# Where layer norms, a reload and two gelus stand in the queues of a macaron transformer block

## The chip, the core and the metric

The kernel runs on one core of one Trainium2 chip. The metric is the device time of one execution in microseconds (us); less is better. Engines are named as in the profile: PE is TensorE (PEld its weight loads), DVE is VectorE, ACT is ScalarE, POOL is GpSimd, and SP is the engine that issues nearly all of the DMAs.

## The reference

One block of 2048 tokens with 512 features: half a gated MLP, causal attention with 16 heads of 32, and the same half MLP again. Every part is preceded by a layer norm without learnt weights. The MLP's weights come as 4-bit codes with one scale per 32 values, and both MLPs use the same weights.

```python
x = x + 0.5 * ffn(layernorm(x), gate_codes, gate_scales, up_codes, up_scales, down_codes, down_scales)
x = x + attn(layernorm(x), w_qkv, b_qkv, w_out, b_out)
x = x + 0.5 * ffn(layernorm(x), ...)          # the same weights again

def ffn(x, ...):                               # hidden width 4096
    gate, up = x @ Wg.T, x @ Wu.T              # Wg, Wu, Wd dequantised from the codes
    inter = gelu_tanh(gate) * up
    return inter @ Wd.T
def layernorm(x): return (x - mean(x)) / sqrt(var(x) + 1e-5)
```

All of it is float32.

## The kernel before, in words

The program is written out in one order by hand: the Python code emits instructions one after another, each goes to the end of its engine's queue, and no scheduler moves it. A line that is emitted earlier therefore stands earlier in its engine's queue and ahead of everything else that this engine has to do. Waits between engines are semaphores.

**The products.** Matrix products are done by Strassen-like schemes with seven half-size products in place of eight. Their sums are made by DVE, ACT and POOL around PE, out of seven rotating PSUM banks (pool `ps_one`, tag `one`) and one further bank (`ps_acc`).

**Transposition.** A product needs the normalised tokens with features on partitions. So each tile of 128 tokens is normalised by ACT (`normalize`: line 146, tile `xn`; in the second MLP's second half line 953, in place in tile `xl`), transposed by four PE instructions (line 155 into `pt_f` or `pt_a`; line 961 into `pt_later`), and copied out of its bank by ACT (line 156 into `xT`; line 962). Tiles `xn` and `xl` have two buffers each.

**First MLP, `ffn(1, ...)`.** Groups g = 0 to 7 of 512 hidden units; in each, `slot(...)` runs fourteen products for the gate (`pg`, line 339) and the up projection (`pu`), over a pair of blocks of 512 tokens. Token blocks 0 and 1 are normalised at the very start. Blocks 2 and 3 are normalised and transposed inside the second slot (`slot(g, second, 0, [], [], 1, late)`): after each product one group of the list `late` is emitted, and its first nine groups come from `staggered(n2, n3)`. In a slot ACT also copies products 1 and 5 out of their banks (lines 378 and 390) and applies the gelu to the four gate results (line 359), each after a DVE addition (line 381 for the first, `c`; then 392, 396, 399).

**Between the first MLP and attention.** `norms_behind` builds the same staggered list for attention's blocks 0 and 1; its groups stand behind the last fourteen pieces of the down projection (`po`, line 438).

**Second MLP, `second_ffn`.** It works on two halves of 1024 tokens. A half is 56 pairs of products (NP = 56; `pair(n, ...)`, n from 0 to 111), each with seven steps for the inner products y = 1, 5, 2, 6, 7, 3, 4. Their results `d`, `f`, `e` (line 746) share banks: y = 6, 7 and 4 accumulate on the bank of y = 1, so PE may start y = 7 only after ACT has copied the bank after y = 6 (`u2`, line 776). `hooks` holds further work by pair and step, `at(half, n, step, ...)`; step k is emitted after inner product k. Down pieces (`pod`, `pof`, `poe`, line 877, with ACT's copy of line 900 and DVE's line 886) are mixed in. Weights for pair n + 4 are fetched by six DMAs of SP when pair n ends (`fetch`, lines 620 to 622).

**The second half's tokens** have lain in DRAM (`away`). Their moments are computed early in the first half. `Later` then reloads the eight tiles (`load`, line 670, 256 KB each), normalises and transposes them while pairs 54 and 55 run. Tile i + 2 is loaded once transposition i has released its buffer.

**The end.** After pair 111 the loop body of n = 112 emits what is left, by hand: the `sums` of the last pair (DVE, line 800), its two `gelus` (ACT, line 803), the `gated` products (DVE, line 812), the sums for the down projection (DVE, lines 856 to 859), and between them the down pieces. A piece is named here by i and q. Left over from group 6 are (4,1), (5,1) and (3,1); fourteen of group 7 follow. Piece (3,1) accumulates on the bank that ACT's copy of (5,1) reads (line 900), and it is the last reader of the tile `s`, which line 856 writes anew.

## Time and profile before

| | |
|---|---|
| median of 3 runs | 3159.78 us (3156.42, 3159.78, 3159.99) |
| the profiled execution | 3161.12 us; its span 3159.3 us, so 1.8 us lie around the span |
| PE busy | 3114.4 us of the span (99%) |
| DVE / POOL / ACT busy | 2055.9 / 1534.8 / 1047.2 us |
| mean granted TensorE clock | 0.997 |

The span is the time that the profile covers, and all positions below are us from its start. "Busy" counts the time in which an engine has an instruction running. The granted clock is the share of full speed at which PE's array was clocked. Rows of a timeline give start, duration, engine, line, operation, and in brackets the idle time ahead of it with what ended it.

### The profile page before, as it was taken

Reading aid. Unit: us, or ns where it says so; the run is one execution under the profiler, and the core shown is the slowest. Engines: PE = TensorE matmul, PEld = TensorE weight load, DVE = VectorE, ACT = ScalarE, POOL = GpSimd, SP = SyncE. Lnnn points to the kernel's source line nnn. Section 1 sums busy time; section 2 is a strip of 40 time slices with the busy share of each in tenths; the row PEclk is TensorE's granted clock in tenths of the full one; section 3 lists DMA queues with packets and bytes.
Section 4 is the critical chain, followed back from the end, with each engine's and each line's share of the span. In section 5 each row is a group of like instructions: output and inputs, shape, how many; then the busy total and the mean of one; then the engine's idle time right before and its main releaser. Section 6 shows DMA issues by size and latency. Waiting matters only on the chain.

```text
span 3159.3 us, 45153 instructions
## 1 busy us (share of the span) xinstructions
PE 3114.4 (99%) x16592; PEld 2006.8 (64%) x16592; DVE 2055.9 (65%) x3182; ACT 1047.2 (33%) x2070; POOL 1534.8 (49%) x1529
## 2 busy tenths in 40 slices
PE   7999999999999999999999999999999999999998
PEld 4556565656565565444335434478888878888887
DVE  6666666666666655655564566687666777666775
ACT  5111111111111122355453456443333343333332
POOL 3767675857667672456564467522232223223221
PEclk9999999999999999999999999999999999999999
DMA  3223122212122220000000000064444445344441
GB/s 140 79 85 114 67 97 90 97 60 97 64 93 80 83 87 24 5 14 9 12 9 7 29 20 11 1 203 130 124 127 129 125 131 171 116 124 129 130 122 61
DMA packets 261293, 260.21 MB, mean 82 GB/s; under 512 B 21216, under 2 KB 225616, under 8 KB 257104
## 3 DMA queue, kind: packets, MB, share of 16 engines
q1 hardware_dynamic: 261072, 257.33, 25.0%
q8 instruction: 131, 2.15, 0.3%
q14 instruction: 90, 0.74, 0.1%
HBM read 176.28 MB, written 79.92 MB: 81 GB/s over the span
## 4 chain that ended last, share of the span: by engine, by line
PE 93%; DVE 2%; ACT 1%; POOL 1%; issue 1%; DMA 1%; SPq 0%; ACTq 0%; POOLq 0%; DVEq 0%
PE po L438 12%; PE d_f L746 12%; PE pg L339 12%; PE pu L339 12%; PE av L1278 7%; PE pod_f L877 7%; PE pm L1206 6%; PE f_f L746 6%; PE pqk L1122 4%; PE pof_f L877 3%; PE e_f L746 3%; PE ps L1357 2%; PE pv L1139 2%; PE pp L1159 2%; PE poe_f L877 2%; PE ps L1366 1%
## 5 line engine op out<-in xcount | busy, mean ns | idle before, releaser
L1391 ACT ACTIVATE pt<-ps 128x512 f32<-128x512 f32 (+3 forms) x608 | 288.2, 528 | 180.8 <-PE ps L1366 118.5
L1206 PE MATMUL pm<-kT,qT 32*128 32x512 f32 (+3 forms) x1280 | 332.3, 572 | 0.0
L1218 DVE TENSOR_REDUCE parts<-pm 128x1 f32<-128x512 f32 x384 | 246.6, 686 | 129.3 <-PE pm L1206 128.9
L746 PE MATMUL d_f<-ys_f,ring 128*128 128x256 f32 x1216 | 319.8, 384 | 10.1 <-DVE o_f L779 5.8
L1415 POOL TENSOR_TENSOR sum<-pt,pt 128x512 f32<-128x512 f32 (+1 forms) x225 | 265.9, 1202 | 95.2 <-ACT pt L1391 88.1
L1366 PE MATMUL ps<-qT,kT 32*128 32x512 f32 (+3 forms) x1280 | 278.3, 536 | 0.0
L746 PEld LDWEIGHTS d_f<-ys_f,ring 128*128 128x128 f32 x1216 | 226.4, 190 | 58.2 <-DVE o_f L779 21.3
L438 PEld LDWEIGHTS po<-wd,inter 128*128 128x128 f32 x1024 | 194.4, 190 | 77.5 <-issue 55.7
L800 DVE TENSOR_TENSOR o_f<-o_f,o_f 128x1024 f32<-128x1024 f32 x128 | 203.6, 1601 | 61.2 <-ACT o_f L785 56.5
L438 PE MATMUL po<-wd,inter 128*128 128x256 f32 x1024 | 241.1, 379 | 0.0
L339 PE MATMUL pg<-xT_f,w 128*128 128x512 f32 x512 | 240.6, 598 | 0.0
L339 PE MATMUL pu<-xT_f,w 128*128 128x512 f32 x512 | 238.0, 592 | 0.0
L892 POOL TENSOR_TENSOR xq<-xq,d_f 128x512 f32<-128x512 f32 x48 | 63.7, 1326 | 314.6 <-DVE xq L886 229.4
L452 POOL TENSOR_TENSOR xq<-xq,d 128x512 f32<-128x512 f32 x124 | 161.8, 1315 | 92.5 <-DVE xq L446 56.2
L892 POOL TENSOR_TENSOR xq_second<-xq_second,d_f 128x512 f32<-128x512 f32 x45 | 61.6, 1370 | 279.6 <-DVE xq_second L886 210.9
L1278 PE MATMUL av<-pt,vals 128*32 128x256 f32 (+1 forms) x2432 | 191.5, 369 | 2.4 <-ACT both L1300 2.3
L393 POOL TENSOR_TENSOR u<-u,u 128x512 f32<-128x512 f32 x64 | 81.9, 1279 | 211.1 <-ACT u L390 210.4
L438 PEld LDWEIGHTS po<-wd,s 128*128 128x128 f32 x768 | 145.5, 190 | 57.9 <-issue 39.2
L438 PE MATMUL po<-wd,s 128*128 128x256 f32 x768 | 181.4, 379 | 0.0
L339 PE MATMUL pg<-xsum,w 128*128 128x512 f32 x384 | 179.6, 597 | 0.0
L800 POOL TENSOR_TENSOR o_f<-o_f,o_f 128x1024 f32<-128x1024 f32 x44 | 119.2, 2709 | 123.8 <-ACT o_f L785 122.7
L339 PE MATMUL pu<-xsum,w 128*128 128x512 f32 x384 | 177.7, 592 | 0.0
(225 smaller groups left out, 6345.9 us busy)
## 6 DMA issues: line engine op xcount, KB each, us to landing
wd_f<-kept SPq DMA_DIRECT2D x112, 256.0 KB
kept<-wd SPq DMA_DIRECT2D x8, 1792.0 KB
xq<-in_x SPq DMA_DIRECT2D x16, 256.0 KB
pk<-in_gate_codes SPq DMA_DIRECT2D x16, 256.0 KB
sc<-in_gate_scales SPq DMA_DIRECT2D x32, 128.0 KB
pk<-in_up_codes SPq DMA_DIRECT2D x16, 256.0 KB
sc<-in_up_scales SPq DMA_DIRECT2D x32, 128.0 KB
pk<-in_down_codes SPq DMA_DIRECT2D x16, 256.0 KB
```

Source lines behind the costliest of these rows:

```text
L339: nc.tensor.matmul(ps, lhsT=a[:, j, :], rhs=b[:, j, :], start=(j == 0), stop=(j == 1))
L438: nc.tensor.matmul(ps[:, j, :], lhsT=a[i][:, k, bass.ts(2 * q + j, P)], rhs=b[i][:, k, :], start=(k == 0), stop=(k == 1),)
L452: adder.tensor_tensor(dst, dst, other, ALU.add)
L746: nc.tensor.matmul(ps[:, k, :], lhsT=fa[k][y], rhs=fb[k][y], start=first and k == 0, stop=True, skip_group_check=True,)
L800: sums.append(lambda: eng.tensor_tensor(dst, dst, other, ALU.add))
L877: nc.tensor.matmul(ps[:, j, :], lhsT=a[:, k, bass.ts(2 * q + j, P)], rhs=wd[:, PLACE[i], k, :], start=new and j == k == 0, stop=True, skip ...
L1206: nc.tensor.matmul(ps[a][:, :n], lhsT=q[r, bass.ts(4 * g + i, P)], rhs=k[r, kb * 512 : kb * 512 + n], start=True, stop=True,)
L1218: nc.vector.tensor_reduce(most, scores, AX.X, ALU.max)
L1278: nc.tensor.matmul(dst_, lhsT=lhsT, rhs=rhs, start=kw.get("start", False), stop=True, skip_group_check=True)
L1366: nc.tensor.matmul(ps[a][:, off:], lhsT=k[r, bass.ts(c, P)], rhs=q[r, g * 512 + off : (g + 1) * 512], start=False, stop=True,)
L1391: nc.scalar.activation(pt[:, a, plain[a] :], ps[a][:, plain[a] :], AF.Exp, scale=scale)
L1415: eng.tensor_tensor(s[:, a, off_2:], one[:, a, off_2:], other[:, a, off_2:], ALU.add)
```

## The change

Three places of the order are edited. The computation, the tiles and the number of instructions stay the same; PE's queue differs only in the place of four of the eight `pt_later` transpositions, the queues of DVE and POOL not at all.

1. `staggered`: the first group normalises two tiles in place of one, and each following group transposes tile i first and normalises tile i + 2 after it. Before, a group normalised tile i + 1 and then transposed tile i. The transpositions keep their groups. The function serves the first MLP (blocks 2 and 3) and attention (blocks 0 and 1).
2. `Later`: the loads of tiles 0 and 1 move from pair 52, step 5 to pair 30, step 0. The eight transpositions, before at steps 0, 2, 4, 6 of pairs 54 and 55, are now at steps 0, 2, 4, 6 of pair 54 and 1, 3, 5, 6 of pair 55. The load of tile i + 2 stays with transposition i. Normalisation i + 1, before in the same step as transposition i, now stands one step behind it.
3. The end: the two gelus of the last pair move behind pieces (5,1) of group 6 and (1,0) of group 7.

```diff
     def staggered(a, b):
         n, t = a.normal + b.normal, a.transposed + b.transposed
-        return [[n[0]]] + [[n[i + 1], t[i]] for i in range(7)] + [[t[7]]]
+        return [n[:2]] + [[t[i], n[i + 2]] for i in range(6)] + [[t[6]], [t[7]]]
...
-            at(0, 52, 5, call(later.load, 0), call(later.load, 1))
+            at(0, 30, 0, call(later.load, 0), call(later.load, 1))
             at(0, 53, 5, call(later.normalize, 0))
             for i in range(8):
-                place = 0, 54 + i // 4, 2 * (i % 4)
-                at(*place, call(later.transpose, i))
+                place = min(2 * i, 13)
+                at(0, 54 + place // 7, place % 7, call(later.transpose, i))
                 if i + 2 < 8:
-                    at(*place, call(later.load, i + 2))
+                    at(0, 54 + place // 7, place % 7, call(later.load, i + 2))
                 if i + 1 < 8:
-                    at(*place, call(later.normalize, i + 1))
+                    at(0, 54 + (place + 1) // 7, (place + 1) % 7, call(later.normalize, i + 1))
...
                     pieces.pop(0)()
-                    for f in sums + gelus:
+                    for f in sums:
                         f()
                     for piece in (pieces.pop(0), pieces.pop(1)):
                         piece()
-                    for f in gated + down_sums[:2]:
+                    for f in gelus + gated + down_sums[:2]:
                         f()
```

## The prediction

> **What bounds the kernel now.** The page says PE, and so does the chain that ended last (its shares by engine):

> ```profile
> PE 3114.4 (99%) x16592; PEld 2006.8 (64%) x16592; DVE 2055.9 (65%) x3182; ACT 1047.2 (33%) x2070; POOL 1534.8 (49%) x1529
> ...
> PE 93%; DVE 2%; ACT 1%; POOL 1%; issue 1%; DMA 1%; SPq 0%; ACTq 0%; POOLq 0%; DVEq 0%
> ```

> The change removes no PE work, so it can only win idle PE time (44.9 us in all) or slow PE time. PE's own list of waits (total, times, longest) names three that lie where the edits are:

> ```profile
> PE pt_f L155 <- ACT xn_f L146: 14.6, 5, 9.4
> ...
> PE d_f L746 <- ACT u_f L776: 4.1, 2, 2.2
> PE pof_f L877 <- ACT d_f L900: 3.5, 2, 2.8
> ```

> 9.4 us of the first is the start of the program, which no edit touches. I then read PE's timeline at each place, and ACT's beside it. Place A, the second slot of the first MLP:

> ```profile
> 56.25 1.13 PE L155 MATMUL pt_f<-ident,xn_f 128*128 128x128 f32 x4 [3.25 <-ACT xn_f L146]
> 57.17 3.62 PE L339 MATMUL pg<-xsum,w 128*128 128x512 f32 x4
> ```
> ```profile
> 49.66 0.82 ACT L146 ACTIVATE xn_f<-xq,nbias_f,rstd_f 128x512 f32<-128x512 f32 x1
> 54.86 0.63 ACT L359 ACTIVATE c<-c 128x512 f32<-128x512 f32 x1 [4.38 <-DVE c L381]
> 55.40 0.80 ACT L146 ACTIVATE xn_f<-xq,nbias_f,rstd_f 128x512 f32<-128x512 f32 x1
> ```

> ACT stood idle for 4.38 us ahead of a gelu whose input DVE had not made, with the next norm queued behind it; PE waited for that norm. The product after it took 3.62 us where its neighbours take 1.88. The table by stretches (length, busy us of PE, PEld, DVE, ACT, POOL, then granted clock) tells why:

> ```profile
> 51.60:55.05 3.45, 1.40 (x4) 0.33 (x2) 3.42 (x6) 0.19 (x1) 0.41 (x1) 1.00 0.45 191
> 55.05:61.90 6.85, 5.65 (x13) 3.33 (x14) 2.38 (x5) 3.85 (x7) 0.00 (x0) 0.50 0.00 0
> ...
> 2570.70:2574.10 3.40, 1.44 (x8) 1.02 (x7) 0.69 (x1) 1.81 (x3) 0.00 (x0) 1.00 0.44 136
> 2574.10:2577.50 3.40, 3.40 (x12) 2.86 (x11) 1.38 (x2) 1.30 (x2) 0.00 (x0) 0.50 0.00 0
> ...
> 2608.20:2611.65 3.45, 1.94 (x9) 1.35 (x8) 3.42 (x5) 0.63 (x1) 0.00 (x0) 1.00 0.00 0
> ```

> A stretch of 3.4 us in which PE is busy for 1.4 is followed by 3.4 or 6.8 us at half clock; one with 1.94 busy (its follower kept clock 1.00) is not. Place C, the reload of the second half's tokens:

> ```profile
> 2556.57 0.81 ACT L953 ACTIVATE xl<-xl,nbias,rstd 128x512 f32<-128x512 f32 x1 [2.81 <-DMA xl<-away]
> 2557.29 0.56 ACT L776 COPY u_f<-d_f 128x512 f32<-128x512 f32 x1
> ```

> ACT waits for a load with the copy `u2` behind it, and PE's y = 7 (2557.90, idle 2.18) needs that copy. Place D, the end:

> ```profile
> 3124.56 0.63 ACT L803 ACTIVATE o_f<-o_f 128x512 f32<-128x512 f32 x1 [4.93 <-DVE o_f L800]
> 3125.82 0.63 ACT L803 ACTIVATE o_f<-o_f 128x512 f32<-128x512 f32 x1 [0.63 <-DVE o_f L800]
> 3126.35 0.58 ACT L900 ACTIVATE d_f<-pof_f 128x512 f32<-128x512 f32 x1
> ```
> ```profile
> 3126.98 3.68 PE L877 MATMUL pof_f<-wd_f,s_f 128*128 128x256 f32 x8 [2.79 <-ACT d_f L900]
> ```

> The copy of piece (5,1), whose product was out at 3122.3, waits behind both gelus; piece (3,1) waits for it and then runs at half clock.

> [...]

> **The change, part by part.** The method: replay each place with the rows' own durations. ACT issues the next instruction 0.48 to 0.54 us after a copy or gelu starts, 0.7 us after a norm; a PE transposition takes 0.47 us, 0.6 after a wait; a product of the first MLP 1.72; an inner product of the second 0.86, a down piece 1.73.

> *A, `staggered` in the first MLP.* Norm 1 comes ahead of the gelu, at 50.4, into ACT's idle time: transposition 1 runs at 52.85, as soon as PE gets there. The gelu still comes at 54.86, since DVE is busy without a break from 46.0 to 54.8, and behind it stand now copy 0 (55.40) and norm 2 (55.9 to 56.7). PE arrives at transposition 2 at 55.07: **a new wait of 1.7 us takes the place of the 3.25**. Norms 3 to 7 are each done 1 us or more before their transposition; the `u4` copies move back by 0.1 us at most. PE now needs, from 49.5 to the slot's end, 1.06 (the wait for norm 0, unchanged) + twelve products × 1.72 + 8 × 0.47 + 0.2 + 1.7 = 27.4, against 82.35 − 49.5 = 32.85. **Gain 5.45.** It lasts: DVE's row at 75.69 waits for PE (0.36), so DVE and then POOL and SP shift along with it. Ends: 3.7, if the new wait throttles the clock for one window (half of 3.41 = 1.7), and 6.3, if DVE's addition comes a little sooner.

> *B, `staggered` before attention.* PE runs from 1165.95 to 1193.88 without a wait, the norms being ready. Norm 4 now follows the scales by one group, but copy 2 (1182.1) stands ahead of it and its scale is made by 1181.7. **0**, between −0.3 and +0.5.

> *C, the loads.* The two loads of pair 52 cost SP 1.04 us at 2532.91, with a weight fetch behind them that waits for its slot until 2539.69 anyway; at pair 30 what is behind them is needed three pairs later. 0 both times: loads 0 and 1 were never late. What counts is the shift of the norms. Replayed from 2549.43: loads 2 to 7 leave SP when they did (load 2 at 2553.17, behind six weight fetches) or sooner, and take the 3.2 to 4.4 us of the chain's rows. `u2` no longer stands behind a load, so the waits of 2.18 and 1.96 go, and with them 3.40 us at half clock (1.7). New waits come, since a norm one step ahead must follow that step's ACT copy: transposition 1 waits 0.55, 2 waits 0.4 for its load, 4 waits 0.5, 6 waits 0 to 0.45 for its load (behind the fetch of pair 58), and 7 waits 1.4, because norm 7 shares its step and follows the bank copy of y = 4. Before: 2.18 + 0.54 + 0.37 + 1.96 + 1.7 = 6.75. Now 3.0. Transposition 7 comes at 2575.5, not at 2579.5. After it DVE is busy almost without a break from 2580.8 to 2615 and sets the pace, beginning with line 629, which waits for the last copy; so its whole run moves with it. **Gain 3.9**, between 2 and 5.

> *D, the end.* ACT copies (5,1) at 3122.4 and (1,0) at 3124.1; the first gelu starts at 3124.6 as before, since its sum is ready at 3124.53. Piece (3,1) starts at 3124.02, right after (1,0), at full clock, and is out at 3125.75, not 3130.68. Then DVE is next: line 856 follows the two gated products at 3127.1 instead of 3130.70, and the rows from there to line 858 keep their lengths, so piece (5,0) starts at 3132.7, not 3136.28. PE waits 0.7 ahead of (2,0), which needs the first gated product, and about 1.5 each ahead of (6,0) and (5,0). **Gain 3.6**, between 1.9 (one throttled window) and 4.2.

> Sum: 5.45 + 0 + 3.9 + 3.6 = 12.9. The profiled execution took 3161.12 us, 1.34 above the median of 3159.78; taken from the median this gives **3146.9**, rounded to 3147. A measurement of this kernel tells about 0.2%, 6.3 us, from no change.

> **The rivals.**

> 1. *The new waits throttle the clock.* A's wait of 1.7 leaves a window with 1.7 busy, and D's two of 1.5 about the same: between the 1.44 that throttled and the 1.94 that did not. [...] Each costs up to 1.7; one or two give 3148.5 to 3150.5. Chance 0.32.
> 2. *A part returns nothing*, for instance C, if every wait for `u2` turns into a wait for a load, or D, if DVE is held by something I don't see: gain 7 to 9.5, 3150.5 to 3153. Nothing speaks for it but the number of my steps. Chance 0.11.
> 3. *The loads decide, and it is slower.* In C every transposition from 2 on waits for a load that starts only when a buffer is free. If the weight fetches stretch the six loads, PE pays each excess. At 6.6 us instead of 3.2 to 4.4 the whole gain of 12.9 is gone; at 8.5 the kernel is 11 us slower, 3171. Against it: the DMA engines are busy for 0.4 to 0.6 of those stretches, and the same six loads behind the same fetches took at most 4.41. Chance 0.04.
> 4. *The norms don't get ahead*, because a wait for a buffer of `xn` holds them where they were: within 2 us of 3159.8. Only two buffers exist, but norm i + 2 stands behind copy i, which is after the buffer's last reader. Chance 0.03.

> **How the numbers follow.** All parts as worked: 0.50. Rivals as given. Faster by over 0.2%: 0.50 + 0.32 + 0.07 of rival 2 = 0.89; slower 0.04 (rival 3); within 0.2% the rest, 0.07. The range reaches from 3142 (A, C and D at their better ends, 2.6 more, and the spread of the runs, whose lowest is 3.4 below the median) to 3153.5 (rivals 1 and 2).

> **What would show it.** A: the wait ahead of the second transposition gone, one below 2 us ahead of the third, the next slot's first gate product near 77 and not 82.35. C: no wait for line 776; waits of 1.5 or less ahead of `pt_later`, the largest ahead of the last; that one some 9.5 us earlier in the span, of which 4 are C's own. D: (3,1) taking 1.9 us, line 856 about 3.6 us sooner against the last pair. PE's rows between 1166 and 1194 only shifted. The prediction is wrong in its core if ACT still idles with a ready norm or copy behind a gelu or a load, or if half-clock stretches remain at A or D.

## The result, and the profile after

The changed kernel takes **3149.03 us** (median of 7 executions, 3147.86 to 3151.93) against 3159.99 us for the kernel before on the same chip (7 executions, 3156.42 to 3162.92). The ratio is 0.997, with a 95% interval from 0.9960 to 0.9979: a small gain, 10.96 us by the medians. The profiled execution took 3148.55 us with a span of 3146.7. Line numbers of `kernel.py` are one higher than before up to about line 960.

The page's engine line, and the shares of the chain that ended last:

```profile
PE 3106.7 (99%) x16592; PEld 2005.8 (64%) x16592; DVE 2054.1 (65%) x3182; ACT 1046.7 (33%) x2070; POOL 1532.9 (49%) x1529
...
PE 93%; DVE 3%; POOL 1%; ACT 1%; issue 1%; DMA 1%; SPq 0%; ACTq 0%; POOLq 0%; DVEq 0%
```

PE is still the bound. It has the same 16592 instructions and is busy for 7.7 us less, though no product was removed: most of that is products that no longer run at half clock. Before, the clock was 0.50 from 55.04 to 61.87, from 2574.08 to 2577.49 and from 3127.04 to 3130.45, and PE was busy for 12.44 us of this; at full clock half of that, by my estimate, would be saved: 6.2 us. After, the clock is 1.00 at all three places. The rest of the 12.6 us by which the span fell is idle PE time.

PE's list of waits after the change (total, times, longest, in us):

```profile
PE pt_f L155 <- ACT xn_f L146: 11.6, 4, 8.7
PE d_f L747 <- DVE o_f L780: 5.7, 5, 2.3
...
PE pt_later L962 <- ACT xl L954: 2.9, 5, 1.4
...
PE pod_f L878 <- issue: 1.7, 1, 1.7
...
PE poe_f L878 <- DVE inter_f L813: 1.1, 1, 1.1
PE pof_f L878 <- DVE inter_f L859: 1.0, 1, 1.0
```

The waits for `u_f` (4.1 us before) are gone, and the 2.8 us wait for ACT's copy of piece (5,1) too. In their place stand shorter ones, for norms of `xl` and for DVE at the end. The rows `d_f` for DVE line 780 and `pof_f` for DVE line 859 (1.0) are as they were.

Place A, PE's timeline and then ACT's beside it:

```profile
52.10 0.63 PE L155 MATMUL pt_f<-ident,xn_f 128*128 128x128 f32 x4
52.56 1.88 PE L340 MATMUL pg<-xsum,w 128*128 128x512 f32 x4
56.00 0.75 PE L155 MATMUL pt_f<-ident,xn_f 128*128 128x128 f32 x4 [1.55 <-ACT xn_f L146]
56.58 1.88 PE L340 MATMUL pg<-xT_f,w 128*128 128x512 f32 x4
```
```profile
48.93 1.52 ACT L146 ACTIVATE xn_f<-xq,nbias_f,rstd_f 128x512 f32<-128x512 f32 x2
54.13 0.63 ACT L360 ACTIVATE c<-c 128x512 f32<-128x512 f32 x1 [3.68 <-DVE c L382]
54.67 0.57 ACT L156 COPY xT_f<-pt_f 128x512 f32<-128x512 f32 x1
55.13 0.81 ACT L146 ACTIVATE xn_f<-xq,nbias_f,rstd_f 128x512 f32<-128x512 f32 x1
```

Both norms now come ahead of ACT's wait for DVE, so the second transposition (52.10) finds its tile. The third norm is still behind the gelu; that is the 1.55. The product after it takes 1.88 us, where the kernel before had 3.62.

Place C, ACT's copy `u2` and the norm that waits for its load, now behind the copy; then, on PE, the last of the later transpositions, with the largest wait left there:

```profile
2548.37 0.58 ACT L777 COPY u_f<-d_f 128x512 f32<-128x512 f32 x1 [0.33 <-PE d_f L747]
2550.21 0.81 ACT L954 ACTIVATE xl<-xl,nbias,rstd 128x512 f32<-128x512 f32 x1 [1.26 <-DMA xl<-away]
```
```profile
2569.34 0.75 PE L962 MATMUL pt_later<-ident,xl 128*128 128x128 f32 x4 [1.39 <-ACT xl L954]
```

Place D, PE, then DVE, then POOL:

```profile
3114.07 1.89 PE L878 MATMUL pof_f<-wd_f,s_f 128*128 128x256 f32 x8
```
```profile
3112.09 1.21 DVE L801 TENSOR_TENSOR o_f<-o_f,o_f 128x1024 f32<-128x1024 f32 x1
3113.34 2.22 DVE L801 TENSOR_TENSOR o_f<-o_f 128x1024 f32<-128x1024 f32 x1
```
```profile
3113.21 1.27 POOL L893 TENSOR_TENSOR xq_second<-xq_second,d_f 128x512 f32<-128x512 f32 x1 [14.36 <-ACT d_f L901]
```

Piece (3,1) starts without a wait and at full clock. But DVE's second sum takes 2.22 us, not the 1.23 it took before. POOL's addition of piece (5,1), which used to run at 3127.01 beside an idle DVE, now starts 0.13 us ahead of that sum.

To compare kernels I use three stretches between fixed landmarks of PE's timeline. **A** runs from the first transposition of the second slot to the next slot's first gate product. **C** runs from pair 54's first transposition to the down piece behind the last transposition, which waits 0.69 us for ACT in every kernel (2586.03 before; it lies 6.0 us behind pair 56's first product `d`). **D** runs from the last pair's first product to the last down piece (3117.87 to 3153.65 before). All are in us.

| kernel | A | C | C to D | D | span |
|---|---|---|---|---|---|
| before | 31.82 | 35.74 | 531.84 | 35.78 | 3159.3 |
| before, second profile (e11) | 30.62 | 36.01 | 531.89 | 34.08 | 3155.8 |
| changed | 26.30 | 32.23 | 531.96 | 33.15 | 3146.7 |
| changed, second profile (e10) | 26.30 | 32.14 | 531.79 | 33.15 | 3146.6 |
| e1, `staggered` alone | 26.30 | 35.92 | 532.04 | 35.77 | 3154.7 |
| e2, later tiles alone | 30.84 | 32.25 | 531.82 | 35.71 | 3154.6 |
| e3, gelus alone | 30.74 | 35.74 | 531.92 | 33.15 | 3154.7 |
| e4, addition held back | 26.30 | 32.45 | 532.53 | 32.62 | 3147.5 |
| e5, loads at pair 52 | 26.31 | 32.32 | 531.94 | 33.15 | 3147.3 |
| e6, norms ahead, old places | 30.84 | 31.45 | 533.44 | 34.09 | 3153.2 |
| e7, places only | 30.85 | 34.55 | 531.83 | 35.37 | 3156.0 |
| e8, third norm twice | 28.81 | 32.66 | 531.82 | 33.14 | 3150.6 |
| e9, three waits taken | 24.48 | 31.37 | 533.52 | 32.62 | 3146.2 |
| e12, the same again | 24.48 | 31.26 | 533.52 | 32.60 | 3146.0 |

Between the two first profiles, A gives 5.52, C 3.51 and D 2.63. The start of the program gives 0.72, which is not the change's: the first input arrives at 8.71 and not at 9.43, and it varies from 8.7 to 9.7 over the profiles here. With 0.2 for the stretches between, these make the 12.6 of the spans. PE's rows at B (27.93 us from 1165.95 before, 27.93 us from 1159.70 after) are only shifted.

### The profile page after: what moved, and what is told of

It reads as the page before. It is cut to its first block, busy times and chain, and to the rows that moved or that the text cites. A ratio compares the mean times of both kernels' runs of the same rounds, so it can differ in the third digit from the quotient of the medians.

```text
span 3146.7 us, 45156 instructions
## 1 busy us (share of the span) xinstructions
PE 3106.7 (99%) x16592; PEld 2005.8 (64%) x16592; DVE 2054.1 (65%) x3182; ACT 1046.7 (33%) x2070; POOL 1532.9 (49%) x1529
## 4 chain that ended last, share of the span: by engine, by line
PE 93%; DVE 3%; POOL 1%; ACT 1%; issue 1%; DMA 1%; SPq 0%; ACTq 0%; POOLq 0%; DVEq 0%
PE po L439 12%; PE pu L340 12%; PE d_f L747 12%; PE pg L340 12%; PE av L1280 7%; PE pod_f L878 7%; PE pm L1208 6%; PE f_f L747 6%; PE pqk L1124 4%; PE pof_f L878 3%; PE e_f L747 3%; PE ps L1359 2%; PE pv L1141 2%; PE pp L1161 2%; PE poe_f L878 2%; PE ps L1368 1%
## 5 line engine op out<-in xcount | busy, mean ns | idle before, releaser
L1280 PEld LDWEIGHTS av<-pt,vals 128*32 128x32 f32 x2432 | 53.0, 108 | 195.8 <-issue 167.9
```

The costliest lines, as they stand in the source:

```text
L1280: nc.tensor.matmul(dst_, lhsT=lhsT, rhs=rhs, start=kw.get("start", False), stop=True, skip_group_check=True)
```

## The experiments

My theory was that work which was ready stood behind a waiting instruction in ACT's queue (a norm behind a gelu, the copy `u2` behind a norm that waits for its load, the copy of (5,1) behind gelus), and that part of the price was PE at half clock after the wait. The rivals were that the gain comes from something else in the same edits (earlier loads, other places of the transpositions), or that it is absorbed or depends on the other parts.

**e1, e2, e3: one part each.** Each is the kernel before with one of the change's three edits, and the other two as before.

```diff
 # e1
-        return [[n[0]]] + [[n[i + 1], t[i]] for i in range(7)] + [[t[7]]]
+        return [n[:2]] + [[t[i], n[i + 2]] for i in range(6)] + [[t[6]], [t[7]]]
 # e2
-            at(0, 52, 5, call(later.load, 0), call(later.load, 1))
+            at(0, 30, 0, call(later.load, 0), call(later.load, 1))
...
-                place = 0, 54 + i // 4, 2 * (i % 4)
+                place = min(2 * i, 13)
...
+                    at(0, 54 + (place + 1) // 7, (place + 1) % 7, call(later.normalize, i + 1))
 # e3
-                    for f in sums + gelus:
+                    for f in sums:
...
-                    for f in gated + down_sums[:2]:
+                    for f in gelus + gated + down_sums[:2]:
```

> The kernel before with the edit of `staggered` alone; loads, later norms and gelus as before. Theory (ready work stood behind a waiting gelu in ACT's queue, and the clock fell after it): the second slot of the first MLP ends 5.5 us sooner against its first transposition (26.3 us from there to the next slot's first gate product, not 31.8), with a wait of 1.5 us ahead of the third transposition and no half-clock stretch near 55; PE's stretch between 1160 and 1194 keeps its 27.93; the places C and D show no gain of their own, so the last pair ends 5.5 sooner: about 3154.5. Rival (a shift so early is absorbed, because DVE sets the pace in later stretches): the 5.5 shrink on the way, the time is 3157 to 3160.

> The kernel before with the edits of the second half's loads, norms and transpositions alone. Theory: from pair 54's first transposition to pair 56's first down product 3.5 us are gained (26.2 us, not 29.7), all waits for the copy of line 776 are gone, no stretch there at half clock, waits of 2.9 us in sum ahead of pt_later; the time is about 3156.3. Rival (the gain at this place came only with the shift from A, which moved it against the weight fetches): a gain below 2 or a wait for a load on PE, 3158 to 3160.

> The kernel before with the order of gelus and kept-back pieces in the last pair alone changed. Theory (POOL's addition of piece (5,1) now starts with the copy and runs beside DVE's second sum, which doubles): the sum at line 800 takes 2.2 us, not 1.23, POOL's addition starts within 0.3 us of it, and the last pair gains 2.6; about 3157.2. Rival (the longer sum came from the phase that A and C gave to DVE, not from POOL): the sum takes 1.2 to 1.3 and the gain is 3.6, 3156.2.

Measured against 3159.80 for the kernel before: e1 3156.01 (ratio 0.9990, 0.9983 to 0.9996), e2 3156.29 (0.9987, 0.9979 to 0.9996), e3 3157.64 (0.9994, 0.9985 to 1.0002; by its time alone, e3 is not told from no change). The medians fell by 3.8, 3.5 and 2.2, together 9.5. The table shows each part at its own place and nowhere else: e1 has the changed kernel's A to 0.01 us and its wait of 1.56, e2 its C, e3 its D. The parts do not need each other, and a shift at A is not absorbed on the way: the 2468 us between A and C vary by less than 1.2 us over the profiles.

e1's time fell by 3.8 and not by the 5.5 I expected, though its A is as long as I expected. The reference was at fault: four other profiles with the old `staggered` have A at 30.7 to 30.9, not 31.8. e11 takes that up.

In e3, DVE's second sum is long too, with neither A's nor C's edit in it, so the rival that their shift made it long is out. DVE and then POOL of e3:

```profile
3121.30 2.22 DVE L800 TENSOR_TENSOR o_f<-o_f 128x1024 f32<-128x1024 f32 x1
```
```profile
3121.17 1.27 POOL L892 TENSOR_TENSOR xq_second<-xq_second,d_f 128x512 f32<-128x512 f32 x1 [14.36 <-ACT d_f L900]
```

**e4: the addition held back.** The changed kernel; the addition of piece (5,1) goes into a list, which is emptied behind the addition of piece (3,1).

```diff
+            held = []
...
+                    elif i == 5 and (half, g, q) == (1, NG - 2, 1):
+                        held.append(lambda x22=x22, u5=u[5]: add(x22, u5))
...
+                        while held:
+                            held.pop()()
```

> The changed kernel with one thing more: POOL's addition of the piece (5,1) of the last group of the second half is issued after that of (3,1), so that it can't run beside DVE's second sum. Theory: the sum at line 800 takes 1.23 again, the piece (5,0) starts 1.0 sooner against the last pair's start (D gains 3.6, not 2.6), and the time falls by about 1 to 3148, unless the addition then meets DVE's next row and lengthens that. Rival (the sum is long for another reason, PE's or ACT's traffic): it still takes 2.2, and the time doesn't change.

DVE's timeline of e4:

```profile
3114.58 1.23 DVE L801 TENSOR_TENSOR o_f<-o_f 128x1024 f32<-128x1024 f32 x1
...
3121.97 2.27 DVE L860 TENSOR_TENSOR inter_f<-inter_f,inter_f 128x1024 f32<-128x1024 f32 x1
```

With POOL out of the way the sum takes 1.23 again. That shows POOL's addition as the cause. The gain was half of the 1.0 I expected: D is 32.62, 0.53 shorter. The held-back addition now runs among POOL's later ones (6.91 us without a break from 3121.90), and DVE's line 860 beside it takes 2.27 where the same sum took 1.92 in the changed kernel. Piece (5,0) waits for that sum: 1.38, not 1.02. The time, 3148.75 (ratio 0.9966, 0.9953 to 0.9978), is not told apart from the changed kernel's.

**e5, e6, e7: what at place C gives the gain.** e5 is the changed kernel with loads 0 and 1 back at pair 52. e6 and e7 are the kernel before with half of C's edit each: e6 moves only the norms, e7 only the transpositions and loads 2 to 7. These three, and e8, e11 and e12 below, were executed once each, so I go by their profiles.

```diff
 # e5
-            at(0, 30, 0, call(later.load, 0), call(later.load, 1))
+            at(0, 52, 5, call(later.load, 0), call(later.load, 1))
 # e6
...
-                    at(*place, call(later.normalize, i + 1))
+                    late = place + (i != 3)
+                    at(0, 54 + late // 7, late % 7, call(later.normalize, i + 1))
 # e7
-                place = 0, 54 + i // 4, 2 * (i % 4)
+                place = min(2 * i, 13)
...
-                    at(*place, call(later.normalize, i + 1))
+                    at(0, 54 + place // 7, place % 7, call(later.normalize, i + 1))
```

> The changed kernel with loads 0 and 1 back at pair 52. Theory (the early loads give nothing; the norms' places do): place C unchanged, 26.2 us from pair 54's first transposition to pair 56's first down product, the same waits within 0.2. Rival (the earlier loads bring C's gain): 1 to 3.5 us more at this place.

> The kernel before with each later norm one step after its former place (the fourth stays in its step) so that the copy `u2` of that step comes ahead of it; transpositions and loads stay where they were. Theory (the copy behind a norm that waits for its load is what costs): the waits for line 776 (2.18 and 1.96) go, the clock stays full there, and most of C's gain, 2.5 us or more, is there without new places for transpositions. Rival (the closer spacing of the transpositions or the earlier loads bring the gain): less than 1 us.

> The kernel before with the transpositions and loads 2 to 7 at the changed kernel's places, but each norm in the step of the transposition ahead of it, as before, and loads 0 and 1 as before. Theory (the norm that waits for its load holds up the copy): waits for line 776 of about 2 us remain, PE falls to half clock at least once, and the place gains less than 1 us. Rival (the places bring the gain): 3 us or more.

e5: C is 32.32. Earlier loads give nothing. e6: C is 31.45, **4.3 us less than before and 0.8 less than in the changed kernel**; all waits for line 776 are gone. The place of the norm behind the step's copy is the whole gain, and the new places of the transpositions cost some of it back. (Three transpositions change place, and not four: those of tiles 4, 5 and 6; tile 7's stays at step 6 of pair 55.) With transposition 6 at step 5, norm 7, one step behind it, shares step 6 with transposition 7 and stands behind the bank copy of y = 4, which makes the 1.39. e7: C is 34.55, 1.2 less (under 1 expected); one wait for the copy is left and is longer. PE, then ACT, of e7:

```profile
2557.05 1.15 PE L746 MATMUL d_f<-ys_f,ring 128*128 128x256 f32 x4 [3.01 <-ACT u_f L776]
```
```profile
2555.71 0.81 ACT L953 ACTIVATE xl<-xl,nbias,rstd 128x512 f32<-128x512 f32 x1 [3.65 <-DMA xl<-away]
2556.43 0.57 ACT L776 COPY u_f<-d_f 128x512 f32<-128x512 f32 x1
```

The norm waits for its load, and the copy that PE needs stands right behind it, as in the kernel before.

But e6 did not keep what it won: from C to D it takes 533.44 us, 1.6 more than the others, and its D is 1.7 shorter than before though nothing was changed there. Both are the clock. Two stretches of e6, one after the other (length, busy us of PE, PEld, DVE, ACT, POOL, granted clock):

```profile
2602.90:2606.30 3.40, 1.23 (x6) 0.75 (x4) 3.37 (x6) 0.44 (x1) 0.00 (x0) 1.00 0.00 0
2606.30:2609.70 3.40, 3.31 (x8) 2.68 (x9) 2.41 (x5) 0.59 (x1) 0.00 (x0) 0.50 0.10 28
```

In the first lies PE's wait of 2.26 us for DVE line 779, which the kernels before and after have as well, at full clock. At D it is the other way round: e6 has the wait of 2.79 us ahead of piece (3,1), and then runs on at full clock.

**e8: a longer wait.** The changed kernel with the third norm of place A issued twice on ACT; the values stay the same.

```diff
+                    if (phase, tb, i) == ("f1", 2, 2):
+                        nc.scalar.activation(xn[i], tiles[i], AF.Identity, bias=nbias[:, i : i + 1], scale=rstd[:, i : i + 1])
```

> The changed kernel with the third token tile's norm in the second block of the first MLP issued twice; its result is unchanged, so that the wait ahead of the third transposition grows from 1.55 to about 2.2 us. It prices a longer wait here. Theory (a wait of about 2 us that lies in one window of 3.4 halves the clock for a window, as the wait of 1.96 did in the kernel before): a stretch of 3.4 us at half clock follows, the slot costs 0.7 + up to 1.7, 26.9 to 28.7 us from the first transposition. Rival [...]: clock 1.00 throughout, 0.7 more and no further loss.

PE's timeline, and the stretch in which the wait lies with the one after it:

```profile
57.81 0.75 PE L157 MATMUL pt_f<-ident,xn_f 128*128 128x128 f32 x4 [2.40 <-ACT xn_f L148]
58.40 3.35 PE L342 MATMUL pg<-xT_f,w 128*128 128x512 f32 x4
```
```profile
55.25:58.65 3.40, 1.00 (x6) 0.78 (x6) 2.54 (x5) 3.37 (x6) 0.00 (x0) 1.00 0.00 0
58.65:62.05 3.40, 3.40 (x7) 1.39 (x6) 0.00 (x0) 1.74 (x4) 0.00 (x0) 0.50 0.00 0
```

The wait grew by 0.85 and the slot by 2.51 (28.81 against 26.30). The other 1.66 is the half-clock stretch. So a wait of 2.40 us that lay whole in the first of these stretches (55.41 to 57.81) was followed by half clock, and the changed kernel's 1.55 was not, in both of its profiles.

**e11: the kernel before once more.**

> The kernel before once more, to see whether its half-clock windows are the kernel's or the run's. Theory (a wait of some length halves the clock for one or two windows of 3.4 us[...]): waits unchanged (3.25 at A, 2.2 and 2.0 to 2.3 at C, 2.79 at D), but the number or place of half-clock windows differs from the first profile; place A is 30.8 us long with one window, 31.8 with two. Rival (the windows belong to the kernel's own order): the same windows, A 31.8 again.

The waits are the same within 0.2 us (3.25 at A; 2.38 and 1.98 at C; 2.79 at D), and the half-clock stretches differ: 3.41 us at A, not 6.83, and none at D. A is 30.62, D 34.08, the time 3157.53. The rival is out: which waits are followed by half clock differs from one execution to the next. Two pairs of stretches of e11, each one with a wait and the one after it: the wait at D, then the 1.98 at C:

```profile
3120.83:3124.24 3.41, 1.48 (x7) 0.95 (x5) 3.34 (x4) 0.95 (x2) 0.00 (x0) 1.00 0.35 98
3124.24:3127.65 3.41, 2.56 (x12) 2.27 (x13) 1.47 (x3) 1.29 (x3) 1.29 (x1) 1.00 0.00 0
...
2567.89:2571.30 3.41, 1.43 (x7) 0.95 (x6) 0.69 (x1) 1.59 (x3) 0.00 (x0) 1.00 0.56 193
2571.30:2574.71 3.41, 3.41 (x11) 2.77 (x11) 0.69 (x1) 1.13 (x3) 0.00 (x0) 0.50 0.01 5
```

The first wait is followed by full clock, the second by 3.41 us at half clock. In the first profile of before, half clock begins at 55.04, 2024.53, 2574.08 and 3127.04 and lasts 6.83, 6.83, 3.41 and 3.41 us. The last two starts are 552.96 us apart, which is 162 times 3.4133; the other distances are 577 and 161 times 3.4133. I call the steps of this grid windows. The whole wait at D, 2.79 (3124.19 to 3126.98), falls into the window that ends at 3127.04. In e11 the half-clock windows begin at 55.67 and 2571.29, 737 times 3.4133 us apart; laid on from there, a boundary falls at 3124.25 and cuts the wait at D (3122.30 to 3125.09) into 1.95 and 0.84.

**e9, e10, e12: the three waits that the profile after shows, taken away.** e9 is the changed kernel with (a) the first gelu of A's slot issued after the first transposition and the third norm, (b) e6's places at C, (c) e4's held-back addition. e10 is the changed kernel, on the same chip. e12 is e9's kernel once more.

```diff
# (a); (b) and (c) as in e6 and e4
                         elif i == 2:
...
                             tt(c11, ps, u2, ALU.add)
-                            done(11, c11)
+                            held11 = len(groups) > 11 and m == 0 and phase == 1
+                            if not held11:
+                                done(11, c11)
...
                             run(groups.pop(0))
+                        if i == 2 and held11:
+                            done(11, c11)
```

> The changed kernel with three things more: in the second slot of the first MLP the first gelu is issued after the first transposition's copy and the third norm; the later transpositions go back to their places of before, with the norms a step ahead (the fourth in its step), which takes the last norm from behind the copy of its own step; and POOL's addition of piece (5,1) is held back as in the fourth experiment. Theory (each of the three takes away a wait that the profile after shows): 1.55 us less from the first transposition to the next slot's first gate product (24.75, not 26.30), 0.8 less from pair 54's first transposition to the down piece that follows the last one (31.45, not 32.23 to 32.66), 0.5 less at the end; 2.9 in all, about 3146. Rival (the waits return elsewhere, because DVE sets the pace after both places or a window falls to half clock): 0 to 1.2 less, 3148 to 3149.

> The changed kernel once more, on the same chip as the one with three waits taken away, so that the two can be compared: its three places as in its first profile (26.30, 32.2 to 32.7 and 33.15 us), about 3149. If half-clock windows come and go with the place of a wait in the window, its waits of at most 1.67 us should still bring none.

> The kernel with three waits taken away once more. Its first profile had a half-clock window after the wait of 2.26 us ahead of a down product 26.4 us behind the landmark of place C (2600.73), which the kernel before and the changed one had at full clock behind the same wait. Theory (the place in the window decides, and differs from run to run): the wait is 2.26 again, the window may be gone, and from the landmark of C to the last pair it is then 531.8 to 532.0 us, not 533.5. Rival (the shift of place C put the wait there for good): 533.5 again.

e9 takes 3146.75 us (ratio to before 0.9958, 0.9945 to 0.9970), e10 3150.24 (0.9969, 0.9957 to 0.9981), the kernel before 3160.35 beside them. The medians are 3.5 apart, but the intervals overlap; the profiles are surer. A is 24.48, 1.82 less: the wait of 1.55 is gone, and 0.27 more with it. C is 31.37, about 0.8 less, D 32.62, 0.53 less. That is 3.1 in all (2.9 expected), and 1.6 of it was lost between C and D, as in e6: in e9 and again in e12 the wait of 2.26 lies within one window. In the eleven profiles other than these three C to D takes 531.79 to 532.53 us; in the eight of them whose grid could be laid, a boundary cuts that wait. Since e12 shows the loss a second time, it stays open whether the shift of C has put the wait there for good. In e9 and e12 half clock begins at 2601.08 and 2601.21, behind the wait, which ends at 2600.73 and 2600.55, and lasts 3.41 us. In e6 it begins at 56.54 and at 2606.30, 747 times 3.4133 us apart. e10 repeats the changed kernel's A, C and D within 0.1 us, at full clock in all three.

## Why the prediction was right

The direction and the mechanism held at A, C and D; one term at D was mis-sized. The number alone would not show this: 3149.03 also lies in the band of rival 1 (3148.5 to 3150.5), and it takes the profiles, with full clock at all three places, to tell that rival from the smaller D.

- **A** was worked out as 5.45 and the profiles show 5.52, with the new wait at 1.55 (1.7 forecast) and the next slot's first product at 76.10 ("near 77"). But 1.0 to 1.2 of the 5.5 is the second half-clock window of the one execution that I had. Against the other old profiles the gain is 4.3 to 4.5. One sign that the forecast named for being wrong did come: ACT still idles, for 3.68 us, with a copy and the ready third norm behind the gelu at 54.13. The forecast's own account of A had them there, with the new wait of 1.7 as the price; e9 shows that taking the gelu out of the way brings 1.82 more.
- **B**: 0 forecast, 0.00 measured.
- **C** was 3.9 and is 3.51. The forecast's own terms, 6.75 less 3.0, make 3.75; 3.9 comes out only with the wait ahead of transposition 6 taken as none. The new waits add up to 2.90 (3.0 forecast), none is for line 776, the largest is ahead of the last transposition (1.39). Against 3.75, 0.24 is missing, and one wait more accounts for it: there are now five and not four, and each costs some 0.28 us more than its idle time. Of this, 0.16 lies ahead of the transposition (2545.06 to 2546.66 is 1.60 with 0.58 idle, where products follow each other at 0.86) and 0.12 behind it (2551.67 − 2551.08 is 0.59 after a wait, 0.47 without). e6 shows that 0.8 more was to be had by leaving the transpositions where they were; the forecast counted the wait of 1.4 that their new places bring, but did not ask what the old places would give.
- **D** was 3.6 and is 2.63. This is **the term that was mis-sized, by 1.0**. The step that failed is "the first gelu starts at 3124.6 as before, since its sum is ready at 3124.53", that is, that DVE's three sums keep their lengths. I followed ACT's copy of (5,1) to PE, which waits for its bank, but not to POOL, which adds the same copy: the addition moved with it, from beside an idle DVE to beside DVE's second sum (1.23 to 2.22). e3 and e4 show it. The waits after that came out as 1.08, 1.67 and 1.02 (0.7 and twice 1.5 forecast), and (3,1) at 1.89 as forecast. And, as at A, part of the 2.63 is the one execution: it carried a half-clock window behind the 2.79 us wait. Of the six profiles with the old order at D, four have that window (D from 35.4 to 35.8) and two do not (34.08 and 34.09); against these two the gain is 0.93.
- **The sum.** 12.9 was taken from the median, though it had been worked out in an execution 1.34 above it that carried four half-clock windows at the places of the edits (two at A, one at C, one at D). e11 has two there. The forecast of 3147.0 lies 2.0 below the measured 3149.03: D's 1.0, C's 0.4, and the rest, which I put down to this base without having shown it.

**The rivals.** The first, that new waits throttle the clock, did not happen in either profile of the changed kernel; in e8, 0.85 us more did it at A. The third, that the loads decide, cost what the forecast had put down for it and no more: in the changed kernel ACT waits 1.26 and 1.62 us for loads, and behind these norms PE waits 0.21 and 0.20 us ahead of transpositions 2 and 6 (0.4 and up to 0.45 forecast). The second came in part: DVE was held at D by something not seen, POOL's addition, but this took 1.0 of D and not the whole. The fourth found nothing.

## What to carry to other kernels

In an in-order queue, an instruction that waits charges everything behind it (at A of before, ACT's idle time of 4.38 us ahead of the gelu held back a norm, and PE waited 3.25 us for that norm); so put what is ready, and what the bound engine needs next, ahead of it. When a step is moved earlier, follow every consumer of its result, not only the one on the critical path: another engine's work comes earlier with it and may collide. And take a second profile before subtracting from one: here two profiles of the same kernel had two and four half-clock windows at the places in question, and spans 3.5 us apart, as much as a whole part that was being sized.

## What the runs showed of the hardware

```profile
2013.87:2017.28 3.41, 1.94 (x17) 1.20 (x10) 3.34 (x9) 0.59 (x2) 3.13 (x5) 1.00 0.00 0
2017.28:2020.69 3.41, 1.40 (x12) 0.72 (x10) 0.28 (x1) 2.01 (x8) 1.88 (x4) 0.50 0.00 0
2020.69:2024.10 3.41, 3.41 (x31) 1.24 (x26) 1.71 (x5) 2.42 (x9) 1.84 (x3) 0.50 0.02 5
```

In the first of these PE is busy for 1.94 us and idle for 1.47, and half clock follows. In before, a half-clock window with 1.23 us idle (2024.53 to 2027.94) was followed by a second there. PE runs attention's products at this place, many of them on 32 partitions; what makes the difference is open.
